# Layer 3's offset and modulation rows of images 0 to 5 as four products of 192 columns in four column strips, with one tanh over 128 partitions and four transfers

## The chip, the core and the metric

The kernel runs on one core of a Trainium2 chip. The metric is the device time of one execution in microseconds. All tensors are float32. TensorE multiplies, VectorE and ScalarE do the work between products, GpSimd does some elementwise products, and SyncE (SP) issues most transfers.

## What is computed

Four residual layers are applied to 8 images of 384 channels and 32 x 32 points. The change is in layer 3, an attention whose keys and values are read at shifted points (deformable attention). For each image and each of three groups of 128 channels, a small convolution of the queries gives a map `off` on a 16 x 16 grid; one product with a 3 x 128 matrix turns it into three rows: two offsets and one modulation.

```python
q = einsum('bchw,oc->bohw', x, q_w)
off = conv(q.reshape(B * 3, 128, H, W), dw_w, stride 2, 5x5, depthwise)
off = gelu(batchnorm(off + dw_b))
om = einsum('bchw,oc->bohw', off, pw_w)                 # pw_w is 3 x 128
offset, modulation = om[:, 0:2], sigmoid(om[:, 2:3])
offset = tanh(offset) * (1 / H_off, 1 / W_off) * 2
x_s = grid_sample_bilinear(x, offset + reference_points) * modulation
k, v = split(einsum('bchw,oc->bohw', x_s, kv_w))
out = proj(softmax(q k^T * scale) v) + proj_b
```

With three groups of 256 grid points, an image has 768 columns of `off`, and so 3 rows of 768 numbers.

## The kernel before

**Stages.** Layer 0 (convolutions and attention) fills the first half of the time. Then layers 1, 2 and 3 run image by image. In the loop over images 0 to 6, layer 1 of image b + 1 (large products: `ph` at L1584 and `y` at L1605) is cut into units, and these are laid between the steps of layers 2 and 3 of image b. `layers(b)` is a generator that yields an estimate of idle time at each step; when enough has gathered, the next unit of layer 1 is issued. So the order of TensorE's queue is fixed when the program is built, and most of it is layer 1's products with layer 2 and 3's products in between. The last image runs in a tail of its own.

**The steps around the change**, in `layer3`, for image b:

1. Queries `pq` (L1767) go to SBUF as `q`. `offsets` (L1861, L1863) forms the 25 taps of `off` on VectorE, and ScalarE applies Gelu to it (L1784).
2. For images 0 to 5 the product `pom` (L1794) multiplies `off` (128 channels by 768 columns) with three columns of weights, `pw3[:, :, 0]`. `pw3` holds each of the three weight columns 128 times, as 128 x 3 x 128. [...] there are two products, of 512 and 256 columns, both into rows 0 to 2 of `po`.
3. ScalarE applies tanh to these 3 rows of 768 (L1796), with a scale for each row from `half3` (1, 1 and 0.5; the sigmoid of the modulation is finished later from its tanh), and writes `oms`.
4. One transfer puts `oms` into `om_dram[b]` in HBM (L1797), and three transfers read each row back, repeated over all 128 partitions, as the tiles `om` (L1800). All four are issued on SP.
5. `sample` turns these tiles into bilinear weights: VectorE adds the reference points (L1881), ScalarE forms `wt` for each of eight blocks of the image (L1904, L1907; one more pass over the column tile at L1887 and L1890), GpSimd multiplies the two directions (L1908), and TensorE sums the sampled image with them: `xsb` and `xs` (L1913).
6. `attend` forms keys and values (L1932, L1943), scores, exponentials and the output `pf` (L2115).

Behind the products `pom`, TensorE's queue holds the rest of layer 1's hidden products `ph` and twelve products of `y`; then it comes to `xsb`. On ScalarE the coefficients `cb` (L1566) of the next image stand ahead of the tanh, and two `hd` (L1594) behind it. On SP the load of the next image's x (L171) stands behind the `om` loads.

Images 6 and 7 take another way (`moved`, L1872 and L1873): they multiply with a weight column repeated 128 times, so the result is on all partitions at once and no transfer is needed.

**Names that are used later.** A float32 product on TensorE runs as two passes; a group of matmuls in the trace counts passes. "128*3" in a row of the trace is the size of the weights in use: 128 rows by 3 columns. A product whose weights have at most 32 columns can be placed in one of four strips of 32 columns of the array, and its result then lies on the 32 partitions of that strip. The gate logits of layer 1 (`plog`, L1312) are written that way: four products with 128 x 32 weights into partitions 0 to 31, 32 to 63 and so on.

Of the kernel before, what the change touches and what calls it, by code (L numbers as in the profile page):

```python
# [8 lines left out]
AF = mybir.ActivationFunctionType  # L9
# [5 lines left out]
P = 128  # L15
# [20 lines left out]
NPAIR3, HS, LS, NG = 3, 16, 256, 3  # L36
# [19 lines left out]
def tile_kernel(ctx: ExitStack, tc: tile.TileContext, i: dict, out: bass.AP):  # L56
    nc = tc.nc
# [9 lines left out]
    def big(name):  # L67
        return ps_big.tile([P, N], F32, tag="big", name=name)
# [6 lines left out]
    def evac(dst, src):  # L75

        flip[0] ^= 1
        if flip[0]:
            nc.scalar.copy(dst, src)
        else:  # L80
            nc.vector.tensor_copy(dst, src)  # L81
# [19 lines left out]
    def gn_start(x, tag, c, st):  # L101

        if st is None:
            st = small.tile([P, 2 * KC, 6], F32, tag="gn_st", name=f"st_{tag}")
        for h in range(2):
            nc.vector.bn_stats(st[:, 2 * c + h, :], x[:, c, h * HALF : (h + 1) * HALF])
        return st
# [30 lines left out]
    def gn_finish(st, tag, psum):  # L138

        return gn_scale(*gn_spread(gn_mean(st, tag), tag, psum), tag, psum)  # L140
# [5 lines left out]
    def affine(dst, src, ss):  # L146
        nc.scalar.activation(dst, src, AF.Identity, bias=ss[:, 1:2], scale=ss[:, 0:1])
# [90 lines left out]
    def rows_of(t, r0, r1):  # L238

        return t.rearrange("p (e h w) -> p h e w", e=2, w=W)[:, r0 // 2 : r1 // 2]  # L240
# [26 lines left out]
    with ExitStack() as pa:  # L267
# [254 lines left out]
        for n, (u, kind, s) in enumerate(work):  # L522
            k, h = divmod(u, 2)
# [36 lines left out]
            for p in passes:  # L560
                j, x = p
                c0, c1 = max(0, 1 - x), W - max(0, x - 1)
                for q in range(nq):
# [3 lines left out]
                    elif kind == "y":  # L567
                        g, j, w = s, q, slice(0, 64)
# [4 lines left out]
                    for r, rs in enumerate(quads):  # L573
                        nc.tensor.matmul(  # L574
                            banks[r][cols[q]].rearrange("p (h w) -> p h w", w=W)[:, :, c0:c1],
                            lhsT=cws[rs, c, 2 * h + g, x, w],
                            rhs=src[rs, :, c0 + x - 1 : c1 + x - 1],
                            start=(p == passes[0]), stop=(p == passes[-1]),
# [63 lines left out]
    scale = HD0 ** (-0.5)  # L642
# [98 lines left out]
    with ExitStack() as pb:  # L741
# [269 lines left out]
        for k in range(2):  # L1011
            qs = slice(k * HALF // 2, (k + 1) * HALF // 2)
            for m in range(KC):
                for c in range(KC):
                    nc.tensor.matmul(
                        pos[m][:, qs], lhsT=wo0[:, c, m * P : (m + 1) * P],
                        rhs=atts[B - 1][:, c, HALF:][:, qs], start=(c == 0), stop=(c == KC - 1),
# [62 lines left out]
    with tc.If(redo > 0):  # L1080
        with ExitStack() as pb:
# [5 lines left out]
            for v, nm in enumerate(("wq0", "wk0", "wv0")):  # L1087
                t = wb.tile(list(i[nm].shape), F32, name=f"{nm}_e")
# [6 lines left out]
            with tc.For_i(0, B) as bi:  # L1095
# [11 lines left out]
                for t in range(NT8):  # L1107
                    pv = big(f"pv_e{t}")
                    for c in range(KC):
                        nc.tensor.matmul(  # L1110
                            pv[:, :C], lhsT=act[2][:, c, t * P : (t + 1) * P],
                            rhs=w_in[2][:, c, :], start=(c == 0), stop=(c == KC - 1),
# [8 lines left out]
                for v in range(2):  # L1121
                    ts = qp.tile([P, NPAIR0, N], F32, tag=f"qk{v}", name=f"qk{v}_e")
                    for pr in range(KC):
                        for h in range(2):
                            pq = big(f"pq{v}_e{pr}_{h}")[:, :HALF]
                            for c in range(KC):
                                nc.tensor.matmul(
                                    pq, lhsT=w_in[v][:, c, pr * P : (pr + 1) * P],
                                    rhs=rows_of(act[v][:, c, :], h * H // 2, (h + 1) * H // 2) if v == 0
                                    else act[v][:, c, h * HALF : (h + 1) * HALF],  # L1130
                                    start=(c == 0), stop=(c == KC - 1),
# [8 lines left out]
                for pr in range(NPAIR0):  # L1140
                    qt, kt = qks[0][:, pr, :], qks[1][:, pr, :]
                    for h in range(2):
                        pav = big(f"pav_e{pr}_{h}")[:, :HALF]
                        for j, r in enumerate(HR):
                            hd = 2 * pr + j
                            pt = qp.tile([P, NT8, HALF], F32, tag="pt", name=f"pt_e{pr}_{h}_{j}")
                            for qc in range(4):
# [3 lines left out]
                                for kh in range(2):  # L1151
# [3 lines left out]
                                        start=True, stop=True,  # L1155
# [3 lines left out]
                                p = pp.tile([P, N], F32, tag="p", name=f"p{nm}")  # L1159
# [14 lines left out]
                            for kc in range(NT8):  # L1174
                                nc.tensor.matmul(
                                    pav[64 * j : 64 * j + 64, :],
                                    lhsT=vt[:, kc, 2 * hd : 2 * hd + 2, :].rearrange(
                                        "p a b -> p (a b)"
                                    ),
                                    rhs=pt[:, kc, :],  # L1180
                                    start=(kc == 0),
                                    stop=(kc == NT8 - 1),
# [5 lines left out]
                for m in range(KC):  # L1188
                    for h in range(2):
                        hs = slice(h * HALF, (h + 1) * HALF)  # L1190
                        po = big(f"po_e{m}_{h}")[:, :HALF]
                        for c in range(KC):
                            nc.tensor.matmul(
                                po, lhsT=wo0[:, c, m * P : (m + 1) * P], rhs=att[:, c, hs],
                                start=(c == 0), stop=(c == KC - 1),
# [3 lines left out]
                    out=o_dram[bass.ds(bi, 1)].rearrange("o p c n -> p (o c) n"), in_=oe  # L1199
# [25 lines left out]
    def load_w(name, t=None):  # L1225
        t = room_w(name) if t is None else t
        nc.sync.dma_start(out=t, in_=i[name])
        return t


    def vbank(name):
        return ps_v.tile([P, HALF], F32, tag="v", name=name)
# [21 lines left out]
    pl = Pools(pd, "d")  # L1254
# [233 lines left out]
    om_dram = dram.tile([B, 3, NG * LS], F32, name="omd")  # L1488
# [258 lines left out]
    def layer3(pl, b, xt, put, general):  # L1747

        st = None
        for c in range(KC):  # L1750
            st = gn_start(xt, f"d3_{b}", c, st)
        yield 3.0
        ss = gn_finish(st, f"d3_{b}", vbank)
        yield 5.0

        h3 = pl.img(f"h3_{b}").rearrange("p c n -> p (c n)").rearrange(
            "p (t c n) -> p t c n", t=NT8, c=KC
        )
        for c in range(KC):
            affine(h3[:, :, c, :], xt[:, c, :].rearrange("p (t n) -> p t n", t=NT8), ss)  # L1760
        yield 3.0
        q = pl.img(f"q_{b}")
        for m in range(KC):
            pq = big(f"pq3_{b}_{m}")
            for h in range(2):
                for c in range(KC):
                    nc.tensor.matmul(  # L1767
                        pq[:, h * HALF : (h + 1) * HALF], lhsT=wq3[:, c, m * P : (m + 1) * P],
                        rhs=h3[:, h * NT8 // 2 : (h + 1) * NT8 // 2, c, :],
                        start=(c == 0), stop=(c == KC - 1),  # L1770
                    )
            evac(q[:, m, :], pq)
            yield 0.0

        xT = h3.rearrange("p t c n -> p t (c n)")
        for t in range(0, NT8, 2):
            evac(rows_by_channel(xT, t), turned(b, h3, t))
            yield 0.4

        off = pl.flat([P, NG, HS, HS], f"off_{b}")  # L1780
        for n in offsets(off, q, range(NG)):
            yield 0.9 if n == 1 else 1.35
        offf = off.rearrange("p g h w -> p (g h w)")
        nc.scalar.activation(offf, offf, AF.Gelu, bias=bo3, scale=so3)  # L1784
        yield 3.0

        yield None

        om = []
        if b < B - 2:  # L1790

            po = big(f"pom_{b}")
            for k in (slice(0, 512), slice(512, 768)):
                nc.tensor.matmul(po[:3, k], lhsT=pw3[:, :, 0], rhs=offf[:, k], start=True, stop=True)  # L1794
            t = pl.flat([P, NG * LS], f"oms_{b}")
            nc.scalar.activation(t[:3], po[:3, : NG * LS], AF.Tanh, scale=half3)  # L1796
            nc.sync.dma_start(out=om_dram[b], in_=t[:3])  # L1797
            for r in range(3):
                t = pl.one([P, NG * LS], f"om{r}", f"om{r}_{b}")
                nc.sync.dma_start(out=t, in_=om_dram[b, r : r + 1].to_broadcast([P, NG * LS]))  # L1800
                om.append(t)
            yield 7.0
        else:
            om = [pl.one([P, NG * LS], f"om{r}", f"om{r}_{b}") for r in range(3)]
            for r in (1, 0, 2):
                moved(b, r, offf, om[r])
                yield 0.3

        def accumulators():
            xsb, xs2 = big(f"xsb_{b}"), vbank(f"xs2_{b}")  # L1810
            return [xsb[:, :LS], xsb[:, HALF : HALF + LS], xs2[:, :LS]]

        xs = yield from sample(
            b, xT, om, accumulators, lambda t, n: pl.flat([P, NG, n], f"wt_{b}_{t}"),
            lambda: pl.flat([P, NG, LS], f"xs_{b}"),
        )
        yield from attend(pl, b, xt, put, general, q, xs)
# [4 lines left out]
    def turned(b, src, t):  # L1822

        px = big(f"px_{b}_{t}")
        for k in range(2):
            for c in range(KC):
                nc.tensor.transpose(  # L1827
                    px[:, k * HALF + c * P :][:, :P], src[:, (t + k) % src.shape[1], c, :], ident
                )
        return px.rearrange("p (t n) -> p t n", t=2)[:, :, :C].rearrange(  # L1830
            "p t (c q) -> p t c q", c=KC
        )

    def rows_by_channel(xT, t):
        return xT[:, t : t + 2, :].rearrange("p t (q c) -> p t c q", c=KC)
# [32 lines left out]
    def moved(b, r, offf, dst):  # L1868

        po = big(f"pom_{b}_{r}")  # L1870
        for k in (slice(0, 512), slice(512, 768)):
            nc.tensor.matmul(po[:, k], lhsT=pw3[:, r, :], rhs=offf[:, k], start=True, stop=True)  # L1872
        nc.scalar.activation(dst, po[:, : NG * LS], AF.Tanh, scale=1.0 if r < 2 else 0.5)  # L1873
# [393 lines left out]
    for b in range(1, B):  # L2267
# [10 lines left out]
        if b + 2 == B:  # L2278
            with tc.issue_after(ahead["load"].ins):
                load_w("w2", w2)  # L2280
                b2, wp3, pb3, dw3, bn3, pw3 = (
                    load_w(n) for n in ("b2", "wp3", "pb3", "dw3", "bn3", "pw3")
                )
                ref3, npos, half3, same = (load_w(n) for n in ("ref3", "npos", "half3", "same"))
# [51 lines left out]
    with tc.If(redo3 > 0):  # L2336
        with ExitStack() as pe:
            pl = Pools(pe, "g")
            with tc.For_i(0, B) as bi:
                xt = pl.img("x_g")  # L2340
                nc.sync.dma_start(
                    out=xt, in_=x2_dram[bass.ds(bi, 1)].rearrange("o p c n -> p (o c) n")
# [28 lines left out]
def _layouts(a):  # L2371
    import numpy as np

    f = np.float32
    L = {}
# [10 lines left out]
    w = np.zeros(B * C * N + 2 * W, f)  # L2386
# [3 lines left out]
    w = np.zeros((P, KC, 4, 3, 80), f)  # L2390
# [73 lines left out]
        [a[f"L3_conv_{n}"] for n in ("dw_b", "bn_w", "bn_b", "bn_mean", "bn_var")], axis=1  # L2464
    )

    L["half3"] = np.array([[1.0], [1.0], [0.5]], f)
    L["pw3"] = np.repeat(a["L3_conv_pw_w"].T[:, :, None], P, axis=2)
    lin = np.linspace(0.5, HS - 0.5, HS, dtype=f) / f(HS) * f(2.0) - f(1.0)
    ref = np.stack([np.repeat(lin, HS), np.tile(lin, HS)])  # L2470
# [27 lines left out]
```

## Time and profile before

| What | Before |
|---|---|
| Median of 3 runs | 3402.43 us (3401.05 to 3407.64) |
| The profiled execution | 3404.2 us |
| Its span (first to last instruction) | 3402.4 us |
| Granted TensorE clock, mean | 0.993 |
| TensorE busy in the span | 3323.7 us |
| `pom` of images 0 to 5 (L1794) | 24 passes, 12 of 512 and 12 of 256 columns |
| tanh of them (L1796) | 6 instructions, 0.892 us each |
| Write of the rows (L1797) | 6 issues, 0.259 us each |
| Loads of the rows (L1800) | 18 issues, 0.319 to 0.426 us each |

How to read it: the profile is one execution, and its durations belong to that execution's own time, not to the median of the runs. Matmuls are pipelined and their ends are modelled, so their busy time overlaps, and the distance from one start to the next says more than a duration. A row of the timeline gives the start and the length in microseconds, the engine, the line, the operation, what it writes and reads, the shape and how many instructions were merged; in brackets at the end stands how long the engine had been idle before, and what ended that. PE is TensorE's matmul, PEld its weight load, DVE VectorE, ACT ScalarE, POOL GpSimd, and SPq the transfers that SP issues.

### The profile page before, as it was taken

Reading aid. Unit: us, or ns where it says so; the run is one execution under the profiler, and the core shown is the slowest. Engines: PE = TensorE matmul, PEld = TensorE weight load, DVE = VectorE, ACT = ScalarE, POOL = GpSimd, SP = SyncE. Lnnn points to the kernel's source line nnn. Section 1 sums busy time; section 2 is a strip of 40 time slices with the busy share of each in tenths; the row PEclk is TensorE's granted clock in tenths of the full one; section 3 lists DMA queues with packets and bytes.
Section 4 is the critical chain, followed back from the end, with each engine's and each line's share of the span. In section 5 each row is a group of like instructions: output and inputs, shape, how many; then the busy total and the mean of one; then the engine's idle time right before and its main releaser. Section 6 shows DMA issues by size and latency. Waiting matters only on the chain.

```text
span 3402.4 us, 44870 instructions
## 1 busy us (share of the span) xinstructions
PE 3323.7 (98%) x18481; PEld 1447.5 (43%) x18481; DVE 1749.1 (51%) x2990; ACT 1300.0 (38%) x1519; POOL 205.1 (6%) x238
## 2 busy tenths in 40 slices
PE   6989999999999999999899999999999999999989
PEld 2333434343434343435344444444444444444443
DVE  8952232323232323233566585565855658658765
ACT  5655444444444445434222323223232232222341
POOL 2100000000000000000000100101002010020121
PEclk9999999999999999999999999999999999999999
DMA  9973121212111121113710110101101011010000
GB/s 356 298 227 81 27 81 26 69 39 60 48 55 51 46 62 43 65 37 104 275 56 22 36 47 30 56 22 36 42 34 56 22 36 41 36 56 22 0 19 38
DMA packets 87411, 234.56 MB, mean 69 GB/s; under 512 B 21928, under 2 KB 22152, under 8 KB 80410
## 3 DMA queue, kind: packets, MB, share of 16 engines
q1 hardware_dynamic: 85034, 223.30, 20.3%
q10 hardware_dynamic: 1248, 4.72, 0.4%
q8 instruction: 149, 2.44, 0.3%
q0 software_dynamic: 912, 3.53, 0.3%
q14 instruction: 68, 0.56, 0.1%
HBM read 146.33 MB, written 75.59 MB: 65 GB/s over the span
## 4 chain that ended last, share of the span: by engine, by line
PE 49%; DVE 2%; ACT 0%; POOL 0%; issue 0%; DMA 0%; DVEq 0%; POOLq 0%; ACTq 0%
PE y L1605 14%; PE ph L1584 14%; PE pf L2115 4%; PE pq L1767 3%; PE pw L1738 3%; PE pav L1987 3%; PE s L1961 2%; PE pk L1932 1%; DVE off L1863 1%; PE pv L1943 1%; PE xsb L1913 1%; PE pw_last L2176 1%; PE xs L1913 0%; PE px L1827 0%; PE plog L1312 0%; PE pom L1794 0%
## 5 line engine op out<-in xcount | busy, mean ns | idle before, releaser
L912 ACT ACTIVATE p<-s 128x1024 f32<-128x1024 f32 x512 | 496.3, 1021 | 365.8 <-PE s L905 365.6
L920 PE MATMUL pav<-p,vt 64*64 64x512 f32 x4096 | 496.3, 588 | 0.0
L1584 PE MATMUL ph<-h,w_sb 128*128 128x512 f32 x1104 | 487.3, 596 | 4.3 <-ACTq L1080 4.1
L1605 PE MATMUL y<-hd,w_sb 128*128 128x512 f32 x1080 | 485.4, 597 | 0.8 <-DVE hd L1570 0.8
L905 PE MATMUL s<-qk,qk 48*64 48x512 f32 x2944 | 355.8, 592 | 0.0
L1584 PEld LDWEIGHTS ph<-h,w_sb 128*128 128x128 f32 x1104 | 208.0, 191 | 261.3 <-issue 254.2
L1605 PEld LDWEIGHTS y<-hd,w_sb 128*128 128x128 f32 x1080 | 199.2, 190 | 231.8 <-issue 221.7
L881 DVE COPY ta<-pav 128x512 f32<-128x512 f32 (+1 forms) x65 | 44.3, 682 | 482.8 <-PE pav L920 482.8
L920 PEld LDWEIGHTS pav<-p,vt 64*64 64x64 f32 x4096 | 172.9, 133 | 267.4 <-issue 259.6
L1594 ACT ACTIVATE hd<-ph,b_sb 128x512 f32<-128x512 f32 x180 | 122.6, 681 | 255.8 <-PE ph L1584 255.8
L574 PE MATMUL pk<-xs,cws_sb 32*32 32x496 f32 (+3 forms) x3840 | 182.3, 596 | 36.4 <-DMA xs<-in_xs_dram 24.5
L1863 DVE SCALAR_TENSOR_TENSOR off<-q,dw_sb,off 128x225 f32<-128x225 f32 (+4 forms) x441 | 215.6, 545 | 2.6
L1726 DVE SCALAR_TENSOR_TENSOR y<-h,tap,y 128x961 f32<-128x961 f32 (+1 forms) x168 | 203.1, 1229 | 0.5
L905 PEld LDWEIGHTS s<-qk,qk 48*64 48x64 f32 x2944 | 111.3, 133 | 208.5 <-issue 184.0
L81 DVE COPY qk<-pq 128x512 f32<-128x512 f32 x46 | 31.8, 692 | 254.4 <-PE pq L258 254.4
L1978 ACT ACTIVATE p<-s 128x1024 f32<-128x1024 f32 x96 | 93.4, 1021 | 162.1 <-PE s L1961 152.6
L1570 DVE TENSOR_TENSOR hd<-hd,cb 128x512 f32<-128x512 f32 x180 | 122.6, 686 | 44.5 <-ACT hd L1594 37.4
L574 PEld LDWEIGHTS pk<-xs,cws_sb 32*32 32x32 f32 (+1 forms) x3840 | 75.3, 110 | 141.8 <-issue 56.0
L2047 POOL TENSOR_TENSOR p<-p,p 128x1024 f32<-128x1024 f32 x48 | 113.6, 2368 | 326.2 <-ACT p L1978 267.1
L2115 PE MATMUL pf<-att,wp_sb 128*128 128x512 f32 x288 | 131.3, 601 | 0.0
L905 PE MATMUL s<-ql,ql 48*64 48x512 f32 x1024 | 129.1, 592 | 0.2 <-ACT p L912 0.2
L780 PE MATMUL pv<-wv_sb,g 128*128 128x384 f32 x384 | 127.1, 489 | 0.0
(385 smaller groups left out, 3731.5 us busy)
## 6 DMA issues: line engine op xcount, KB each, us to landing
rqk<-y SPq DMA_DIRECT2D x96, 256.0 KB
g<-rqk SPq DMA_DIRECT2D x96, 256.0 KB
xs<-in_xs_dram SPq DMA_DIRECT2D x56, 384.0 KB
g<-rv SPq DMA_DIRECT2D x48, 256.0 KB
xh<-in_x_dram SPq DMA_DIRECT2D x47, 256.0 KB
o<-ot SPq DMA_DIRECT2D x42, 256.0 KB
x<-in_x_dram SPq DMA_DIRECT2D x21, 512.0 KB
o<-o SPq DMA_DIRECT2D x21, 512.0 KB
```

The source lines that it names most:

```text
L574: nc.tensor.matmul(banks[r][cols[q]].rearrange("p (h w) -> p h w", w=W)[:, :, c0:c1], lhsT=cws[rs, c, 2 * h + g, x, w], rhs=src[rs, :, c0 ...
L780: nc.tensor.matmul(pv[:, :C], lhsT=acts[b][2][:, c, t * P : (t + 1) * P], rhs=w_in[2][:, c, :], start=(c == 0), stop=(c == KC - 1),)
L905: nc.tensor.matmul(s[64 * k : 64 * k + 64, j * HALF : (j + 1) * HALF], lhsT=kt[r, k0 : k0 + 64], rhs=qt[r, h * HALF : (h + 1) * HALF], sta ...
L912: nc.scalar.activation(p, s, AF.Exp, scale=scale)
L920: nc.tensor.matmul(pav[k][64 * j : 64 * j + 64, :], lhsT=vts[b % 2][r, kc, 2 * hd : 2 * hd + 2, :].rearrange("p a b -> p (a b)"), rhs=p[r, ...
L1570: ahead["hd"] = nc.vector.tensor_tensor(hd, hd, state["cb"], ALU.mult)
L1584: ahead["ph"] = nc.tensor.matmul(ph, lhsT=w1[:, e, c, dc * P : (dc + 1) * P], rhs=state["h1"][c], start=(c == 0), stop=(c == KC - 1),)
L1594: nc.scalar.activation(hd, ph, AF.Relu, bias=b1[:, k : k + 1])
L1605: nc.tensor.matmul(y, lhsT=w2[:, e, dc, m * P : (m + 1) * P], rhs=state[h, k], start=(k == 0), stop=(k == NE * KC - 1),)
L1726: nc.vector.scalar_tensor_tensor(d, f, tap2[:, c, t : t + 1], d, ALU.mult, ALU.add)
L1863: nc.vector.scalar_tensor_tensor(d, f, dw3[:, t : t + 1], d, ALU.mult, ALU.add)
L2115: nc.tensor.matmul(pf, lhsT=wp3[:, pr, m * P : (m + 1) * P], rhs=att[:, pr, hs], start=(pr == 0), stop=(pr == NPAIR3 - 1),)
```

## The change

The 768 columns are cut into four parts of 192. Each part is multiplied by itself, into its own 32 partitions of the accumulator: part k goes into partitions 32k to 32k + 31, columns 0 to 191. The weights for this are every twelfth column of the flattened `pw3` (3 x 128 columns): 32 columns, of which 0 to 10 are the first weight column, 11 to 21 the second and 22 to 31 the third. So in each strip the three rows appear repeated, and rows 0, 11 and 22 of a strip are the three wanted. One tanh runs over all 128 partitions and 192 columns, with `half3` now holding a scale for each partition (0.5 for the rows 22 to 31 of a strip). Four transfers then write 3 x 192 numbers each into `om_dram`. The loads behind them, images 6 and 7, and all else stay as they were.

```diff
             po = big(f"pom_{b}")
-            for k in (slice(0, 512), slice(512, 768)):
-                nc.tensor.matmul(po[:3, k], lhsT=pw3[:, :, 0], rhs=offf[:, k], start=True, stop=True)
-            t = pl.flat([P, NG * LS], f"oms_{b}")
-            nc.scalar.activation(t[:3], po[:3, : NG * LS], AF.Tanh, scale=half3)
-            nc.sync.dma_start(out=om_dram[b], in_=t[:3])
+            w = NG * LS // 4
+            for k in range(4):
+                nc.tensor.matmul(
+                    po[32 * k : 32 * k + 32, :w], lhsT=pw3.rearrange("p r m -> p (r m)")[:, ::12], rhs=offf[:, k * w : (k + 1) * w],
+                    start=True, stop=True,
+                )
+            t = pl.flat([P, w], f"oms_{b}")
+            nc.scalar.activation(t, po[:, :w], AF.Tanh, scale=half3)
+            for k in range(4):
+                nc.sync.dma_start(
+                    out=om_dram[b, :, k * w : (k + 1) * w], in_=t[32 * k : 32 * k + 23 : 11]
+                )
             for r in range(3):
                 t = pl.one([P, NG * LS], f"om{r}", f"om{r}_{b}")
                 nc.sync.dma_start(out=t, in_=om_dram[b, r : r + 1].to_broadcast([P, NG * LS]))
...
-    L["half3"] = np.array([[1.0], [1.0], [0.5]], f)
+    L["half3"] = np.where(np.arange(P)[:, None] % 32 > 21, 0.5, 1.0).astype(f)
```

Lines of the changed kernel after this place are seven higher.

## The prediction

> **What bounds the kernel now.** I read busy time per engine first, then the chain of waits, then the stretches between one image's `pom` products and the next.
>
> ```profile
> PE 3323.7 (98%) x18481; PEld 1447.5 (43%) x18481; DVE 1749.1 (51%) x2990; ACT 1300.0 (38%) x1519; POOL 205.1 (6%) x238
> ...
> PE 49%; DVE 2%; ACT 0%; POOL 0%; issue 0%; DMA 0%; DVEq 0%; POOLq 0%; ACTq 0%
> ...
> 1897.70:2111.30 213.60, 213.38 (x631) 97.46 (x630) 136.33 (x201) 61.34 (x84) 19.46 (x16) 1.00 0.11 38
> 2111.30:2324.50 213.20, 213.20 (x632) 97.54 (x631) 135.13 (x200) 62.42 (x85) 19.48 (x16) 1.00 0.11 38
> ```
>
> The chain of waits is TensorE for nearly all of what it lists, with a little VectorE in the tail. The two stretches are whole periods of the image loop (length, then busy time of PE, PEld, DVE, ACT, POOL, the granted clock 1.00, DMA share and GB/s): TensorE is busy for all but 0.2 of 213.6 us, VectorE for 136, ScalarE for 61. So in this loop the time is TensorE's queue, whose order is fixed, and a time taken out of a queue slot is a gain unless something else is late afterwards. The slot in question, image 0, in the timeline (start, length, engine, line):
>
> ```profile
> 1897.73 1.45 PE L1794 MATMUL pom<-off,pw_sb 128*3 128x512 f32 x4
> 1897.91 0.80 ACT L1566 ACTIVATE cb<-w0s,prs,dp 128x512 f32<-128x512 f32 x1
> 1899.12 4.56 PE L1584 MATMUL ph<-h,w_sb 128*128 128x512 f32 x10
> 1899.22 0.89 ACT L1796 ACTIVATE oms<-pom,half_sb 3x768 f32<-3x768 f32 x1 [0.51 <-PE pom L1794]
> 1900.14 0.26 SPq L1797 DMA_DIRECT2D omd<-oms  x1
> 1901.71 1.28 SPq L1800 DMA_DIRECT2D om<-omd  x3
> ```
>
> The ends of matmuls are modelled, so I read from start to start: `pom` holds TensorE from 1897.73 to 1899.12, **1.39 us**. In the other five images it is 1.38 or 1.39. A float32 product runs as two passes (x4 for two products); a pass of 512 columns costs 0.429 us (24 passes of `y`, 1903.51 to 1913.81), so 0.84 ns a column. 768 columns in two passes are 1.28 us, and 0.11 is the change from the full array to a column strip and back.
>
> **Part 1, the products.** Removed: 4 passes in one strip. Added: 8 passes of 192 columns (0.16 us each), two in each of four strips. If strips run side by side this is two rounds, 0.32 us; if not, 8 x 0.16 = 1.28 us as before. Another row of this trace has just this form, the gate logits (L1312): 128x32 weights, four strips, a different stream for each.
>
> ```profile
> 1641.33 2.78 PE L1312 MATMUL plog<-f,gate 128*32 128x512 f32 x24
> 1644.04 1.13 PE L1584 MATMUL ph<-h,w_sb 128*128 128x512 f32 x2
> ...
> 1641.33 0.16 PEld L1312 LDWEIGHTS plog<-f,gate 128*32 128x32 f32 x8 [0.76 <-DVE f L1052]
> 1641.78 0.13 PEld L1312 LDWEIGHTS plog<-f,gate 128*32 128x32 f32 x4 [0.30 <-issue]
> ```
>
> 24 passes of 512 columns take 2.71 us: six rounds of 0.429 (2.57) and 0.14 for the changes of form. Without overlap they would take 10.3. Eight weight loads lie within 0.16 us, so loads of different strips overlap too. For `pom` this gives 2 x 0.16 + 0.15 = **0.47 us**. A second row agrees at the short end: `pbs` (two strips, 16 columns, 4 passes) holds TensorE from 1949.68 to 1949.85, 0.17 us; with 176 more columns in each of two rounds that is 0.17 + 0.30 = 0.47.
>
> A rule speaks against it. The Trainium skill, "TensorE: Matmul & The Clock Gate", Part 3 ("The mechanism"), says that a weight load overlaps matmuls in flight only if its row group differs. Here all strips use all 128 rows. By that rule every pass first waits for its load, 0.11 us by the `plog` rows, so 8 x (0.11 + 0.16) = 2.16 us, +0.77 us an image, +4.6 in all. The `plog` rows contradict it: four loads within 0.13 us in each round, and rounds still 0.43 apart. I take the row. The weights differ from `plog` in one thing, a step of 12 words between columns. The old load had a step of 128 words and took 0.083 to 0.088 us for three columns, so no penalty shows. The second and third product each carry a wait on VectorE for work that finished before the Gelu; a semaphore step of TensorE's queue shows 0.05 us, and I price both at nothing, at most 0.1 us.
>
> Ends for the slot: 0.46 us (pure two rounds and the rest of `pbs`), and 0.79 if the strips pair up only two by two, as the two strips of `pav` do (8 passes of 512 in 1.87 us). Saving 0.6 to 0.93 an image; I take 1.39 - 0.47 = 0.92, over six images **-5.5 us** (ends -3.6 and -5.6).
>
> **Part 2, tanh and its transfers.** None of this is on TensorE, so it costs only if the sampling weights come late.
>
> ```profile
> 1905.73 1.93 DVE L1881 SCALAR_TENSOR_TENSOR om<-om,ref_sb 128x768 f32<-128x768 f32 x2 [0.60 <-DMA om<-omd]
> 1910.76 2.68 POOL L1908 TENSOR_TENSOR wt<-wt,om 128x144 f32<-128x144 f32 x5 [70.75 <-ACT om L1890]
> 1913.38 0.19 PEld L1913 LDWEIGHTS xsb<-wt,h 128*128 128x128 f32 x1 [0.24 <-issue]
> ```
>
> The rows `om` do wait for DMA (0.60 us on VectorE), but the first weight tile leaves GpSimd at about 1911.3 (a fifth of 2.68 us after 1910.76), and TensorE asks for it at 1913.38: 2.1 us of slack; 2.2 in image 1, 2.8 in image 5. With TensorE 0.92 earlier, about 1.2 is left.
>
> Step by step: the products end at 1898.20 instead of 1899.12, but ScalarE runs `cb` until 1898.71, so tanh starts 0.5 earlier, not 0.9. Its length falls with the columns: 768 from PSUM take 0.81 us (L1873) and 1024 take 1.02 (L912), 0.84 ns a column, so 0.89 - 576 x 0.84 ns = 0.41 us. The first write can be issued at about 1899.16 instead of 1900.14. Four issues instead of one: at the 0.26 us of the old write, the last starts 0.78 later; at the 0.43 of the `om` loads, 1.28 later. The loads follow the last write by the old 1.57 us (1900.14 to 1901.71). They are issued at 1901.5 or at 1902.0, that is 0.2 earlier to 0.3 later. Both fit in 1.2 us of slack, so I take **zero**.
>
> In the order of the queues the four writes wait for older transfers on their completion lanes and for tanh, never for each other; only the first `om` load waits for all four. What stands behind them on SP is the next x load, issued 20 us later (1921.87), so it does not care. On ScalarE a shorter tanh lets the two `hd` behind it run earlier. The `half3` load grows from 3 to 128 rows, once, 200 us before its use. On VectorE and GpSimd the order is unchanged.
>
> Here the second rule: "DMA: Bandwidth & Descriptors" (two cost components; "Rules for kernel authors") gives every transfer about 2.0 us fixed and advises to coalesce small ones. Taken one after another, three more writes are 6 us, 5 us later at the loads after the earlier start; less 1.2 slack, a stall of 3.8 an image, and +17 us with the gain counted. But the three `om` loads are issued within 1.28 us, without one waiting for the other's landing: the fixed time is latency, and lies side by side. By the row the sum stays zero.
>
> **Does the gain reach the end?** VectorE waits 9 times, 80 us in all, for `pq` in this loop, so it takes its pace from TensorE afresh in every image. Between `pq` and `pom` nothing changes, and the Gelu ends at 1897.44, before the previous pass ends. What is late next is nothing within 1 us. After image 5 the chain is again TensorE, with VectorE and GpSimd stretches that start from its results, so all of it shifts.
>
> **Sum.** The profiled execution took 3404.2 us (span 3402.4): 3404.2 - 5.5 = 3398.7. The median shown, 3402.43, is 1.8 below that execution, so I forecast **3397.0 us**, 0.16% less. About 0.2% (6.8 us) is what a measurement of this kernel can tell from no change (its three runs lie between 3401.05 and 3407.64).
>
> **Rivals.**
> A, forecast: strips overlap, chain hidden: 3396 to 3399 (3.6 to 5.6 less). For it: the `plog` rows. Chance 0.76.
> B, no net gain: the strips run one after another, or their loads or semaphore steps eat the overlap. Slot 1.2 to 1.5 us: 3401 to 3403; at the rule's 2.16 us, 3407. For it only the stride, the waits between products and passes this short, which no row shows together; against it `plog` and `pbs`. Chance 0.15.
> C, slower: the `om` chain becomes the bound. Place: the first load of `xsb` behind GpSimd's `wt`. Price: if the writes land one behind the other, 3 x 1.57 = 4.7 us, less 1.0 for the earlier start, is 3.7 later; less 1.2 slack it stalls 2.5, less 0.92 gained is +1.6 an image, 3412. It decides only from 2.1 us later than today. Against it: the loads' rows. Chance 0.09.
>
> **How the numbers follow.** Range 3393.5 to 3402.5: A with some 2.5 us of scatter at the fast end, and most of B. Faster by over 0.2% needs 1.3 us more than computed, reachable by scatter alone: 0.22. Within 0.2%: the rest of A and nearly all of B, 0.69. Slower: C, 0.09.
>
> **What would show it.** Right: in the timeline, `pom` x8 of 128*32, next `ph` start 0.45 to 0.55 us after its first; stretches between `pom` of 212.7 and 212.3 us; tanh near 0.41 us; four `omd` issues 0.26 to 0.43 apart; no wait of `xsb` for GpSimd over 0.2 us. Wrong in part 1: passes of `pom` starting 0.16 us apart instead of together. Wrong in part 2: `om` loads after 1904, and TensorE waiting for `wt`.

## The result and the profile after

| What | Before | Changed |
|---|---|---|
| Median of 14 runs each, taken side by side | 3403.56 us (3400.22 to 3408.66) | 3398.51 us (3393.92 to 3400.89) |
| Ratio of the two, with its 95% interval | | 0.9981 (0.9974 to 0.9988) |
| The profiled execution | 3404.2 us | 3399.6 us |
| Its span | 3402.4 us | 3397.7 us |

The changed kernel is 0.19% faster by the ratio. Its interval leaves out 1 and stands for 4.1 to 8.8 us; the two medians differ by 5.05 us. The page of the changed kernel, first the busy times and then the shares of the chain of waits:

```profile
PE 3317.9 (98%) x18505; PEld 1451.5 (43%) x18505; DVE 1749.4 (51%) x2990; ACT 1296.4 (38%) x1519; POOL 205.1 (6%) x238
...
PE 49%; DVE 2%; ACT 0%; DMA 0%; POOL 0%; issue 0%; DVEq 0%; ACTq 0%; POOLq 0%; SPq 0%
```

TensorE has 24 more passes and is busy 5.8 us less; it still sets the time. The same two periods of the image loop (length, then busy PE, PEld, DVE, ACT, POOL, granted clock, DMA share, GB/s):

```profile
1900.28:2113.03 212.75, 212.51 (x636) 97.44 (x635) 136.31 (x201) 60.86 (x84) 19.48 (x16) 1.00 0.11 38
2113.03:2325.31 212.28, 212.28 (x636) 97.50 (x635) 135.09 (x200) 61.78 (x85) 19.48 (x16) 1.00 0.10 38
```

From the first `pom` to the next first `pom`, they were 213.61 and 213.16 us before. All five periods are 0.86 to 0.89 us shorter. The slot of image 0, in the timeline:

```profile
1900.28 0.23 PEld L1795 LDWEIGHTS pom<-off,pw_sb 128*32 128x32 f32 x8 [0.76 <-ACT off L1784]
1900.28 0.57 PE L1795 MATMUL pom<-off,pw_sb 128*32 128x192 f32 x8
1900.45 0.80 ACT L1566 ACTIVATE cb<-w0s,prs,dp 128x512 f32<-128x512 f32 x1
...
1900.78 4.56 PE L1584 MATMUL ph<-h,w_sb 128*128 128x512 f32 x10
1901.16 0.40 ACT L1800 ACTIVATE oms<-pom,half_sb 128x192 f32<-128x192 f32 x1
...
1901.59 2.87 SPq L1802 DMA_DIRECT2D omd<-oms  x4
...
1905.63 1.28 SPq L1807 DMA_DIRECT2D om<-omd  x3
```

From `pom` at 1900.28 to `ph` at 1900.78 the slot is 0.50 us, in all six images, against 1.39: eight weight loads lie within 0.23 us, so the strips do run side by side. Below that the picture is worse than before: the four writes take 2.87 us to issue, and the `om` loads come 5.35 us after `pom` instead of 3.98. What this leaves at the point where TensorE takes the weights over, in image 2:

```profile
2334.50 1.90 DVE L1888 SCALAR_TENSOR_TENSOR om<-om,ref_sb 128x768 f32<-128x768 f32 x2 [2.68 <-DMA om<-omd]
...
2339.52 2.69 POOL L1915 TENSOR_TENSOR wt<-wt,om 128x144 f32<-128x144 f32 x5 [71.92 <-ACT om L1897]
...
2340.08 0.19 PEld L1920 LDWEIGHTS xsb<-wt,h 128*128 128x128 f32 x1 [0.24 <-POOL wt L1915]
```

VectorE idles 2.68 us for the loads. A fifth of GpSimd's row (five instructions, so this stands for the first) ends at 2340.06, and the first weight load of `xsb` starts at 2340.08, with GpSimd named as its releaser: the slack is 0.02 us. Over the six images it is 0.33, 0.26, 0.02, 0.44, 0.46 and 0.46 us; before it was 2.1 to 2.7. In this run nothing is lost, since the load starts 14.77 us after `pom` in every image, but hardly anything is left.

Two questions were open: whether the overlap of strips is the gain, and whether the late loads already cost something. The times below are each beside runs of the kernel before on the same chip; for the first four kernels these have a median of 3405.0 us (37 runs, 3401.5 to 3408.8).

### The profile page after: what moved, and what is told of

It is laid out like the page before. It is cut to its first block, busy times and chain, and to the rows that moved or that the text cites. A ratio compares the mean times of both kernels' runs of the same rounds, so it can differ in the third digit from the quotient of the medians.

```text
span 3397.7 us, 44968 instructions
## 1 busy us (share of the span) xinstructions
PE 3317.9 (98%) x18505; PEld 1451.5 (43%) x18505; DVE 1749.4 (51%) x2990; ACT 1296.4 (38%) x1519; POOL 205.1 (6%) x238
## 4 chain that ended last, share of the span: by engine, by line
PE 49%; DVE 2%; ACT 0%; DMA 0%; POOL 0%; issue 0%; DVEq 0%; ACTq 0%; POOLq 0%; SPq 0%
PE y L1605 14%; PE ph L1584 14%; PE pf L2122 4%; PE pq L1767 3%; PE pw L1738 3%; PE pav L1994 3%; PE s L1968 2%; PE pk L1939 1%; DVE off L1870 1%; PE pv L1950 1%; PE xsb L1920 1%; PE pw_last L2183 1%; PE xs L1920 0%; PE px L1834 0%; PE plog L1312 0%; PE pom L1879 0%
```

## The experiments

### Only the transfers: the old products and tanh, with four writes

```diff
-            nc.sync.dma_start(out=om_dram[b], in_=t[:3])
+            w = NG * LS // 4
+            for k in range(4):
+                nc.sync.dma_start(
+                    out=om_dram[b, :, k * w : (k + 1) * w], in_=t[:3, k * w : (k + 1) * w]
+                )
```

(The diff is against the kernel before.)

> Products and tanh as before, but the rows are written by four transfers of 3 x 192. Theory (the gain is TensorE's slot alone): no gain; the slot of pom stays 1.39 us. The loads of om are issued about 4.0 us after the first write, as in the changed kernel, instead of 1.57, so 2.5 us later than before; against 2.1 to 2.8 us of slack TensorE waits 0 to 0.4 us an image: 3403 to 3406 us. Rival (the gain comes from the part behind the products): faster by some 5 us. For the issue of one write: 0.63 us if its price lies in the cut rows, 0.26 us if it lies in the step of 11 partitions.

Measured: 3404.08 us (12 runs), ratio 0.9997 (0.9988 to 1.0006). There is no gain, and no loss that can be told. No wait of TensorE was left over either, because the loads came much earlier than the expected 4.0 us after the first write. Its transfers on SP, in the timeline:

```profile
1902.96 1.20 SPq L1799 DMA_DIRECT2D omd<-oms  x4
1905.21 1.29 SPq L1804 DMA_DIRECT2D om<-omd  x3
```

and its write issues by tile (count, min/median/max ns):

```profile
L1799 SPq DMA_DIRECT2D omd<-oms x24: 257/262/272, 1903.0 to 2971.1; - x24
```

A write of a quarter of the columns is issued in 0.26 us, just as the whole write was. The three more writes move the loads from 1.44 to 1.57 us after the first write to 2.11 to 2.25: 0.7 us, about the issue time of three writes (0.79). So the writes do not wait for each other's landing, and the 0.63 us and more of each write in the changed kernel does not come from cutting the rows. The destination is the same in both; what differs is the source: partitions 0, 11 and 22 instead of 0, 1 and 2.

### Only the form of the products: all four in one strip

```diff
-                    po[32 * k : 32 * k + 32, :w], lhsT=...[:, ::12], rhs=offf[:, k * w : (k + 1) * w],
+                    po[:32, 256 * k : 256 * k + w], lhsT=...[:, ::12], rhs=offf[:, k * w : (k + 1) * w],
...
-                nc.sync.dma_start(
-                    out=om_dram[b, :, k * w : (k + 1) * w], in_=t[32 * k : 32 * k + 23 : 11]
-                )
+            nc.sync.dma_start(out=om_dram[b], in_=t[:23:11])
```

The eight passes and their weights are those of the changed kernel; tanh runs over 32 partitions of 768 columns, and one write takes rows 0, 11 and 22.

> The same four products of 192 columns with the same 32 weight columns, but all in strip 0, one behind the other; tanh over 32 rows of 768 and one transfer of rows 0, 11 and 22. Theory (side by side is what gains): 8 passes of 0.16 us, a slot of about 1.4 us, and the time of before, 3402 to 3405 us. Rival (smaller products or fewer matmul columns by themselves gain, or the chain behind them): under 3400 us. Issue of the one write: 0.26 us if the price lies in the cut rows, 0.63 us if it lies in the step of 11 partitions.

Measured: 3404.43 us (20 runs), ratio 0.9999 (0.9992 to 1.0005), slot 1.45 to 1.46 us in all images. Its timeline in image 0:

```profile
1896.98 1.19 PEld L1795 LDWEIGHTS pom<-off,pw_sb 128*32 128x32 f32 x8 [0.76 <-ACT off L1784]
1896.98 1.53 PE L1795 MATMUL pom<-off,pw_sb 128*32 128x192 f32 x8
...
1898.44 4.56 PE L1584 MATMUL ph<-h,w_sb 128*128 128x512 f32 x10
```

and its write issues by tile:

```profile
L1804 SPq DMA_DIRECT2D omd<-oms x6: 674/678/807, 1899.5 to 2967.0; - x6
```

The same eight loads now spread over 1.19 us instead of 0.23, and the whole gain is gone. It is the place in four strips that makes it: passes, columns and weights are the same here. Even here the loads stay hidden: eight passes with eight loads take 1.46 us, not 2.16. And a single write of three whole rows costs 0.67 to 0.81 us to issue when the rows lie 11 partitions apart, against 0.26 when they lie next to each other.

### Eight writes: the loads made later still

```diff
             for k in range(4):
-                nc.sync.dma_start(
-                    out=om_dram[b, :, k * w : (k + 1) * w], in_=t[32 * k : 32 * k + 23 : 11]
-                )
+                for j in range(2):
+                    js = slice(j * w // 2, (j + 1) * w // 2)
+                    nc.sync.dma_start(
+                        out=om_dram[b, :, k * w + j * w // 2 : k * w + (j + 1) * w // 2],
+                        in_=t[32 * k : 32 * k + 23 : 11, js],
+                    )
```

> The changed kernel with eight transfers of 3 x 96 in place of four of 3 x 192; the build also lays one y product between the blocks of xsb. Theory (the four writes have used up the slack, to 0.0 to 0.3 us): at 0.63 us an issue the loads of om come 2.5 us later still, TensorE waits for the weights wt some 2.2 to 2.5 us an image, 13 to 15 us in all: 3410 to 3414 us, slower than before. Rival (the transfers are hidden with room to spare): 3397 to 3400 us, as the changed kernel.

Measured: 3426.34 us (4 runs), ratio 1.0057 (1.0040 to 1.0074). That is 21 us over the kernel before and some 26 to 28 over the changed kernel (whose runs were a series of their own), about twice what was expected of the wait alone. The build also issues one product `y` earlier, between two blocks of `xsb`; it stands behind the wait, and in all other runs TensorE's order is that of the kernel before. The timeline in image 2:

```profile
2331.96 5.42 SPq L1804 DMA_DIRECT2D omd<-oms  x8
2338.53 1.28 SPq L1810 DMA_DIRECT2D om<-omd  x3
...
2347.72 0.65 PE L1923 MATMUL xsb<-wt,h 128*128 128x48 f32 x4 [1.72 <-POOL wt L1918]
```

The loads come 7.88 us after `pom`, 2.7 us later than in the changed kernel, and TensorE waits 1.72 us for GpSimd in this image (10.8 us over six). So the chain does set the time from here on. The other half of the loss is in the clock. Stretches of 2 us around that wait (busy PE, PEld, DVE, ACT, POOL, granted clock, DMA share, GB/s):

```profile
2346.00:2348.00 2.00, 0.28 (x4) 0.28 (x3) 1.56 (x3) 2.00 (x6) 0.82 (x2) 1.00 0.00 0
2348.00:2350.00 2.00, 2.00 (x16) 2.00 (x15) 0.35 (x1) 1.37 (x5) 1.86 (x4) 0.71 0.00 0
2350.00:2352.00 2.00, 2.00 (x6) 1.40 (x6) 0.00 (x0) 1.33 (x5) 1.32 (x3) 0.50 0.00 0
...
2354.00:2356.00 2.00, 2.00 (x4) 0.73 (x4) 0.00 (x0) 0.00 (x0) 0.00 (x0) 0.58 0.00 0
2356.00:2358.00 2.00, 2.00 (x17) 1.76 (x16) 0.00 (x0) 0.00 (x0) 0.00 (x0) 1.00 0.04 8
```

After the wait TensorE is busy again, but at half its clock until about 2355.7: some 6.8 us, of which half, 3.4 us, is lost. Images 0 and 1 have the wait (1.74 and 1.64 us) and keep the clock: their periods are 2.0 and 1.9 us longer than in the changed kernel, so up to 0.3 us an image is left for the product that moved. Images 2, 4 and 5 fall to half for some 6.8 us and lose 5.3, 5.4 and 5.5 us; image 3 falls for some 3.4 us and loses 3.7. Together this is 23.8 us. The two spans are 25.3 us apart; the rest is image 0 starting 1.4 us later.

### Three writes, one for each row: the loads made earlier

```diff
-            for k in range(4):
+            for r in range(3):
                 nc.sync.dma_start(
-                    out=om_dram[b, :, k * w : (k + 1) * w], in_=t[32 * k : 32 * k + 23 : 11]
+                    out=om_dram[b, r].rearrange("(k n) -> k n", k=4), in_=t[11 * r :: 32]
                 )
```

Products and tanh are those of the changed kernel; each write takes one row from the four strips.

> The changed kernel with three transfers, one for each row (4 partitions, 32 apart, by 192 columns), so that a load of om waits only for its own row. Theory (the chain is just hidden in the changed kernel, and TensorE's slot is all that counts): the first load is issued about 2.2 us after the first write instead of 3.8 to 4.0, the slack before xsb comes back to 1.5 us or more, and the time stays at 3397 to 3400 us. Rival (the late loads hold the changed kernel back): faster by more than 2 us.

Measured: 3397.40 us (10 runs), ratio 0.9975 (0.9965 to 0.9985). Its transfers in the timeline:

```profile
1903.90 1.70 SPq L1802 DMA_DIRECT2D omd<-oms  x3
1905.71 1.32 SPq L1807 DMA_DIRECT2D om<-omd  x3
```

and its writes by tile:

```profile
L1802 SPq DMA_DIRECT2D omd<-oms x18: 477/483/607, 1903.9 to 2967.8; - x18
```

The loads come 3.12 us after `pom` (at 1902.59) instead of 5.35. The rows of image 0 at the place where TensorE takes the weights over:

```profile
1914.37 2.68 POOL L1915 TENSOR_TENSOR wt<-wt,om 128x144 f32<-128x144 f32 x5 [69.49 <-ACT om L1897]
...
1917.36 0.19 PEld L1920 LDWEIGHTS xsb<-wt,h 128*128 128x128 f32 x1 [0.24 <-issue]
```

The slack is back at 2.3 to 2.6 us over the six images. Yet the periods are 212.73 and 212.29 us, the changed kernel's within 0.02. So the late loads cost the changed kernel nothing: with 2 us of slack or with 0.02, TensorE takes the same time. The two ratios' intervals overlap and come from separate series, so this version is not shown to be faster than the changed kernel; it is the safer one, since its slack is that of before.

### The weights next to each other

```diff
-                    ..., lhsT=pw3.rearrange("p r m -> p (r m)")[:, ::12], rhs=offf[:, k * w : (k + 1) * w],
+                    ..., lhsT=pw3[:, 0, :32], rhs=offf[:, k * w : (k + 1) * w],
```

All three rows are then the first one's; the second and third weight columns are left out.

> The changed kernel with 32 neighbouring weight columns (all of them the first row's) instead of every twelfth; the second and third row are then copies of the first, so the sampled image differs, the work does not. Theory (the step of 12 words makes the weight loads slow): loads of about 0.11 us instead of 0.14 to 0.17, slot of pom 0.47 us or less instead of 0.50, 0.2 us in all over six images, which is too little for the time to show. Rival (the step costs nothing, 192 columns do): loads as now and a slot of 0.50 us.

Measured in a single run: 3397.49 us, with a run of the kernel before beside it at 3406.18; for the time this is too little to tell. The weight loads by tile, first of this kernel:

```profile
L1795 PEld LDWEIGHTS pom<-off,pw_sb x48: 106/108/109, 1898.3 to 2961.0; 128*32 128x32 f32 x48
```

and of the changed kernel:

```profile
L1795 PEld LDWEIGHTS pom<-off,pw_sb x48: 142/156/172, 1900.3 to 2963.1; 128*32 128x32 f32 x48
```

The step of 12 words makes a load about 0.05 us longer (0.156 against 0.108 in the median). The slot falls to 0.46 us, so the step costs 0.04 us an image and 0.2 in all.

### Both kernels again: is there more in the tail?

The gain in the loop is 4.4 us over five periods. In the profiled pair the start of image 0 is 2.5 us later in the changed kernel (1900.3 against 1897.7), and the tail, from the last `pom` to the end, is 2.8 us shorter: 437.5 us before and 434.7 after. The slot of image 5 explains 0.9 of it. Four more single runs, two of each kernel:

> The kernel before, once more, for a second trace. Theory (the change acts only between the pom products of images 0 to 5): the stretches between pom repeat within 0.1 us (213.6 and 213.2), while the start of image 0 (1897.7 before, 1900.3 changed) and the tail after image 5 (437.5 before, 434.7 changed) move by 1 to 3 us by themselves. Rival (the tail's 2 us beyond the slot belong to the change): the tail is 437.5 again to within 0.3 us.

> The changed kernel, once more, for a second trace. Theory (the tail's 1.3 to 2.2 us beyond the slot come from where the half-clock windows of TensorE happen to lie against the work): the loop repeats (212.7 and 212.3), and the first half-clock window of the tail may begin anywhere from 258.3 to 260.0 us after the last pom, so the tail may be 434.6 to 436.6 us. Rival (the change itself shortens the tail): 434.6 to 434.8 us again.

> As the run before: the changed kernel a third time. Theory: a tail of 434.6 to 436.6 us, following the place of the half-clock windows. Rival: 434.6 to 434.8 us.

> The kernel before, a third trace. Theory: a tail of 435.5 to 437.9 us, following the place of the half-clock windows. Rival: 437.5 to 437.9 us, as in its two traces so far.

| Kernel | Run | First two periods | Tail | `pw_last` to `pk` |
|---|---|---|---|---|
| before, again | 3407.67 us | 213.61, 213.17 us | 437.9 us | 18.50 us |
| before, third | 3406.59 us | 213.64, 213.16 us | 437.8 us | 18.42 us |
| changed, again | 3398.40 us | 212.73, 212.28 us | 436.5 us | 18.39 us |
| changed, third | 3397.44 us | 212.75, 212.28 us | 434.2 us | 17.23 us |

(A further run of the kernel before, beside the last three, took 3400.67 us: single times scatter by several us.) The periods repeat within 0.04 us. The start of image 0 does not: it lies at 1897.7, 1900.8 and 1899.8 us in the three traces of the kernel before and at 1900.3, 1897.3 and 1898.6 in those of the changed one, so it scatters whatever the kernel. The tail of the kernel before stays within 0.4 us (437.5 to 437.9); that of the changed kernel moves by 2.3 us, which speaks against the rival that the change itself gives a fixed 434.6 to 434.8. In the tail TensorE waits 3.34 us for ScalarE ahead of `pw_last`, and `pw_last` then begins at half clock. The rows of the changed kernel, again:

```profile
3221.40 18.56 PE L2183 MATMUL pw_last<-y_last,upw 128*128 128x512 f32 x36 [3.34 <-ACT y_last L2175]
3239.79 2.75 PE L1939 MATMUL pk<-xs,wk_sb 128*128 128x256 f32 x12
```

and of its third run:

```profile
3222.76 17.39 PE L2183 MATMUL pw_last<-y_last,upw 128*128 128x512 f32 x36 [3.34 <-ACT y_last L2175]
3239.99 2.75 PE L1939 MATMUL pk<-xs,wk_sb 128*128 128x256 f32 x12
```

The same instructions behind the same wait take 18.39 and 17.23 us. In all eleven traces this stretch is 15.52 us, its length at full clock, plus half of the half-clock time that was still ahead when it started: 3.4 us in the third run, 5.75 in the one above. Three more half-clock stretches follow in the tail. With half of all the half-clock time in which TensorE was busy taken out, the tail is 426.9 to 427.1 us in the five traces with the long slot and 425.4 to 425.9 in the five with the short one (that of the eight writes, with its extra wait, left out): 1.1 to 1.7 us apart, of which the slot is 0.9. So more than half of the tail's extra gain is where half-clock stretches fall, and a changed kernel with a late one has a tail of 436.5, within 0.1 us of what the slot alone gives (437.5 less 0.9). Whether the short slot itself favours the earlier place is not settled: of the same five traces that have it, four have 3.4 to 4.3 us of half clock left and one 5.75; the five without it have 5.0 to 6.0.

## Why the prediction was right

**The slot** was mis-sized by 0.03 us. It was put at 0.47 and is 0.50, so an image gains 0.88 to 0.89 us instead of 0.92, and six gain 5.3 instead of 5.5. "No penalty shows" for the step of 12 words was wrong: packed weights bring 0.46, the predicted slot within 0.01. The old load of three columns could not show it. The waits of the second and third product on VectorE, priced at nothing, cost too little to show: with packed weights the sum comes out without them. The 0.15 us beyond the passes, put down to the change from the full array to strips and back, came out at its size (0.46 less 0.32); that this change is its cause was not tested.

**The rule on row groups** (the Trainium skill, "TensorE: Matmul & The Clock Gate", "The mechanism"), which made it 2.16 us, does not describe these products. With one row group for all, eight loads into four strips lie within 0.23 us, and even in a single strip eight passes with their loads take 1.46. The choice of the `plog` row over the rule was what put the forecast on the right side.

**Tanh** was put at 0.41 us and is 0.40.

**The writes** were the mis-sized term that mattered. They were put at 0.26 to 0.43 us each, from rows whose source lay on neighbouring partitions or in HBM; they are 0.63 to 0.81. The loads follow the last write by 1.67 to 1.83 us, not 1.57. So the loads come 1.2 to 1.4 us later than before, where 0.2 earlier to 0.3 later was predicted, and 0.02 to 0.46 us of slack is left in the profiled execution instead of 1.2. Of the signs named, the four issues 0.26 to 0.43 us apart did not show (their starts are 0.74 apart), and the loads stayed short of the mark for being wrong: 1904 is 6.3 us after `pom`, and they came 5.35 after it. The zero for this part is right, as the three writes by row show with the same periods, but that was luck: the old slack happened to cover an error of more than 1 us. In the third run of the changed kernel image 3 did wait, 0.03 us (14.80 us from `pom` to the `xsb` load instead of 14.77).

**The rule on coalescing** (the Trainium skill, "DMA: Bandwidth & Descriptors", its two cost components and "Rules for kernel authors"), which made it +17 us, was read too hard. The page fits its 2.0 us to transfers that GpSimd issues, and these go out on SP; here they do not add up: three more writes move the loads by 0.7 us, not by 6. What a further write costs is its issue time on SP. The advice to use fewer transfers holds all the same: three writes bring the slack back, eight make the kernel slower.

**The gain reaches the end**: all periods are shorter by the slot, as predicted (212.75 and 212.28 against 212.7 and 212.3). By the sum the profiled execution should have taken 3398.7; it took 3399.6, and the difference of the medians is 5.05 us. That the single profiled times come so close is chance in part, since the start of image 0 and the tail moved by 2.5 and 1.9 us beyond the slots, in opposite directions.

**Rival B** is closed: the slot is nowhere near 1.2 to 1.5. **Rival C** named the right place, the `xsb` load behind `wt`, and with eight writes it is real; but its mechanism, writes that land one behind the other, is not what makes the loads late, and its price lacked the clock. A wait of about 2 us at that place cost up to 5.5 us an image.

## What to carry to other kernels

Small products with at most 32 weight columns are worth cutting into four column strips where TensorE's queue sets the time: two rounds of short passes took 0.50 us in place of 1.39 (worth 0.19% of this kernel). Then follow the result out of the strips: price each transfer by a row whose partitions lie as far apart as its own, and cut transfers along the rows that are read back if that makes fewer of them. Where slack shrinks to tenths, look for the cliff by making the chain later on purpose; on a full TensorE a wait can cost more than its length (here up to 5.5 us for a wait of about 2).

## What was not expected of the hardware

- A write of three rows is issued in 0.26 us from partitions 0, 1 and 2, and in 0.63 to 0.81 us from partitions 0, 11 and 22, whether the rows have 96, 192 or 768 numbers; one row from four partitions 32 apart takes 0.48 to 0.61. Why the step matters was not tried.
- A weight load of 32 columns takes 0.106 to 0.109 us when they lie next to each other and 0.142 to 0.172 at a step of 12 words.
- A wait of TensorE of 1.6 to 2.0 us was followed by half clock in four of six images, for 6.8 us or 3.4. The length agrees with the free-running window of 3.41 us that the Trainium skill states ("TensorE: Matmul & The Clock Gate", "What's actually happening"): two of them, or one. Why images 0 and 1 kept the clock was not tried, but the trace shows a pattern: all its half-clock stretches begin and end on one grid of 3.41 us, and in the grid step that holds the wait TensorE is busy 1.71 and 1.77 us in images 0 and 1, and 1.69, 1.64, 1.56 and 1.38 in images 2 to 5. The split lies at half a step. These are six cases, and it is not the whole rule: in the tail of the changed kernel's third run, half clock follows a step in which TensorE is busy for 2.90 us with products of 64 columns or fewer.
